# A graph network with experts: layer 0's experts from gathered lanes instead of all tokens, and smaller edits beside it

## The chip, the cores and the metric

One core of one Trainium2 chip runs the whole program. The time is device microseconds (us) of one execution; the median of five runs stands for a kernel. Engines are named as in the profile: PE (matrix), PEld (its weight loads), DVE (vector), ACT (scalar), POOL (GpSimd), SP (issues DMAs).

## The reference

N = 3125 nodes with 256 features, E = 50000 edges sorted by destination, all in f32. Four pairs of a graph layer and an expert layer, each added to x. What matters here is the first pair, the first graph half of the second, and the experts of layers 2 and 3:

```
x = x + gnn0(LN(x))      # sum over edges of (h @ W[relation])[src] * weight, by dst
x = x + ffn0(LN(x)):     # 8 experts, each token keeps its best 2
    logits = t @ router.T ; rw, re = top_k(softmax(logits), 2) ; rw = rw / rw.sum
    out = t + sum over the 2 chosen e of rw_e * (gelu(t @ w1[e] + b1[e]) @ w2[e] + b2[e])
x = x + gnn1(...):       # msg = embed[type][src] * (edge_feats @ W_dist) * cutoff ; summed by dst
x = x + ffn2(...)        # 16 experts of 256->512->256, best 2 of 16
x = x + ffn3(...)        # 8 experts of 256->512->256, best 2 of 8
```

## The kernel before

The program has stages. **Stage one** (`stage_one`, 98 to 1892 us of the profile) does layer 0 and the graph half of layer 1 together, one tile of 126 nodes after another, 25 tiles. Then a small stage for layer 1's feed-forward (to 2110 us), layer 2's attention over edges with its 16 experts and the table for layer 3 (to 3197 us), layer 3's maximum over edges (to 3845 us), and layer 3's 8 experts (to the end).

In stage one a tile has 21 windows, each the edges of six nodes. `window` (L874 on) does, for window k: two matmuls of the gathered rows by a weighted 0/1 matrix s (L881, tile `c`, 96 columns), copied out by ACT to `aT` (L885), a matmul of edge features (L888, tile `pw`), and DVE's product `mt = pw * g` (L891), which lets go of the gathered row buffer `g`, of which there are nine; POOL then gathers row k+9 (L136, through the helper `gather`). `build` makes the two matrices of 0/1 columns two windows ahead on DVE: `s0` (L866, 96 wide, times the edge's weight) and `s1` (L868, 32 or 128 wide, times the edge factor of layer 1). `add_up` multiplies each `mt` by its `s1` into one PSUM tile `agg` (L907), which ACT copies to `ag` (L913). After the 21 windows, eight calls of `weigh` multiply `aT` by the relation weights (L920).

The order of work is written out by hand: the stage runs under a manual schedule, so every engine executes in the order of the program text. After each window and each `weigh` call stands one **slot**, `between()`: there are 29 slots a tile. In each slot the `Flow`s of finished pairs of tiles advance by a planned number of steps, and so do a list of background steps (`background`: edge offsets, node ranks for the later layers), weight loads and the zeroing of DRAM tables. A `Flow` has three parts, paced by slots:

```
PARTS = ((route, 22, 25), (experts, 32, 56), (combine, 34, 52))     # part, steps, slots
```

`route` normalises the pair's 2 x 126 tokens, turns them (L950, L951), takes the router's logits (L993) and the best two (`top2_steps`), and adds the second bias (L1012, L1013). `experts` runs **all eight experts on all 252 tokens**: a hidden layer in two halves of two matmuls each (L1029, 252 columns), gelu on ACT (L1031), then for each of the two tiles two matmuls of 256 columns (L1038), and DVE's x = py * comb + x (L1040), where comb is zero for an expert that was not chosen. `combine` does layer 1's graph half and writes the two tables for later layers. After the last tile the remaining Flows run out, one step a slot (the **tail**). All parts take their PSUM from one tag `w` with two buffers (`bank`).

`background` finds each tile's edge range: `begin(t)` gathers rows (POOL), and two slots later `starts` counts on DVE (L584, L586) and multiplies on PE at once (L651). Later it ranks the nodes: per tile three matmuls (L1347 to L1349) and a 0/1 matrix from DVE (L1325), then L1377 with four DVE-built operands (L1373, L1375).

For layers 2 and 3 a planner (`Plan`) orders each engine's instructions from estimated costs. `Experts.loads` issues on SP, expert by expert, the tokens' rows (`ro_x`, L1988) and the two halves of the expert's weights (`ro_w`, L1994, two buffers each); the rows of a chunk of tiles can only be loaded when all of its tokens have been scattered to DRAM (`xg`). `ex2.rest` is a branch for tokens beyond an expert's places (L2072). `attend` reads gathered neighbour rows from nine `g_rows` buffers.

Of the kernel before, what the change touches and what calls it, by code (L numbers as in the profile page):

```python
# [19 lines left out]
P = 128  # L20
# [58 lines left out]

def places(n, chunk):  # L80

    return n * chunk[2] * chunk[3]
# [9 lines left out]
BG_EVERY = 3  # L92


@with_exitstack
def tile_gnn_ffn(ctx: ExitStack, tc: tile.TileContext, a: dict, out: bass.AP):
# [214 lines left out]
    ex = dram.tile([NX, 2 * D], F32, name="ex")  # L311
    tabr = dram.tile([NX, VW], F32, name="tabr")
# [334 lines left out]
    def starts(t, n, pf):  # L647

        for i in range(t, t + n):
            find.count(i)  # L650
        nc.tensor.matmul(pf[:R1, :n], sel[:GC, :], startF[:GC, t : t + n], start=True, stop=True)  # L651
        nc.vector.tensor_scalar(mixI[:R1, t : t + n], pf[:R1, :n], off[:R1], None, op0=OP.add)
# [12 lines left out]
    for i in range(5):  # L665
# [9 lines left out]
        if i == 0:  # L675
            starts(0, 2, ps("tp", [P, 2]))
            first_meta = meta_load(0, wb)
# [39 lines left out]
    def first_zeros():  # L717
        exv = ex.rearrange("(p r) d -> p (r d)", p=TN)
        for c in range(0, NT * 2 * D, ET):
            nc.sync.dma_start(exv[:, c : c + ET], zero[:TN])  # L720
            yield
        nc.sync.dma_start(tab2[NX:, :], zero[: NP - NX, :ZW])
# [65 lines left out]
    def stage_one(late, cp, eb):  # L788
# [67 lines left out]
        def build():  # L856
            k = nxt["s"]
            if k < len(wins):
# [3 lines left out]
                s0 = eb.tile([P, GW], F32, name="s0", bufs=4)  # L862
                a = quarter(j)
                a, m1 = (0, P) if a is None else (32 * a, 32)
                s1 = eb.tile([P, m1], F32, name=f"s1_{m1}", bufs=13 if m1 == 32 else 3)
                nc.vector.tensor_scalar(s0, iota_f[:, :GW], m[:, F_CODE, j : j + 1], m[:, F_NORM, j : j + 1],  # L866
                                        op0=OP.is_equal, op1=OP.mult)
                nc.vector.tensor_scalar(s1, iota_f[:, a : a + m1], m[:, F_DST, j : j + 1], m[:, F_CUT, j : j + 1],  # L868
                                        op0=OP.is_equal, op1=OP.mult)
                sums[k] = s0, s1  # L870
# [3 lines left out]
        def window(k):  # L874
# [5 lines left out]
            for h in range(2):  # L880
                nc.tensor.matmul(pc[:, h, o : o + GW], g[:, h * P : (h + 1) * P], sums[k][0], start=True, stop=True)  # L881
# [8 lines left out]
            mt = mults[t, j] = eb.tile([P, D], F32, name="mt", bufs=11), sums.pop(k)[1]  # L890
            nc.vector.tensor_tensor(mt[0], pw, rows.pop(k)[:, D:], op=OP.mult)  # L891
            fetch_rows()

        ag_of, mults = {}, {}

        def add_up(t, b):
# [4 lines left out]
            for js in together[b]:  # L901
                js = [j for j in js if (t, j) in mults]
                for j in js:
                    a = quarter(j)
                    mt, s1 = mults.pop((t, j))
                    o = agg if a is None else agg[32 * a : 32 * a + 32]
                    nc.tensor.matmul(o, s1, mt, start=not begun, stop=(j == 10), skip_group_check=True)  # L907
                begun = True
            if b == 2:
                q, i = t // 2, t % 2  # L910
                if i == 0:
                    ag_of[q] = eb.tile([P, 2, D], F32, name="ag", bufs=3)
                nc.scalar.copy(ag_of[q][:TN, i, :], agg[:TN])  # L913

        def weigh(t, i):
# [6 lines left out]
            if i == 7:  # L922
                x = x_of[t // 2][:TN, t % 2, :]
# [3 lines left out]
        x_of, e_of = {}, {}  # L927
# [4 lines left out]
        def load_x(q):  # L932
            n = size(q)
            x = x_of[q] = eb.tile([P, 2, D], F32, name="x", bufs=3)
            if n == 1:
                nc.gpsimd.memset(x[:, 0, :], 0.0)
                nc.sync.dma_start(x[:TV, 0, :], a["x"][2 * q * TN :, :])
            else:
                nc.sync.dma_start(x[:TN], a["x"][2 * q * TN : 2 * (q + 1) * TN, :].rearrange("(t p) d -> p t d", p=TN))

        def load_e(q, i):
            n = size(q)
            e = e_of[q, i] = eb.tile([P, 2, D], F32, name=f"e{i}", bufs=1)
            nc.sync.dma_start(e[:TN, :n], rows126(ex, 2 * q, n)[:, :, i * D : (i + 1) * D])
# [29 lines left out]

        def route(q):

            n = size(q)
            x = x_of[q][:TN, :n, :]
            nc.vector.tensor_add(x, x, e_of.pop((q, 0))[:TN, :n])
            yield  # L980
            xn = eb.tile([P, 2, D], F32, name="xn0", bufs=1)[:TN]
# [1531 lines left out]
```

## Time and profile before

| | us |
|---|---|
| median of 5 runs (4242.15 to 4262.89) | 4250.05 |
| the profiled execution | 4246.1 |
| its span, first to last instruction | 4244.4 |
| PE busy, share of span | 2721.8, 64% |
| DVE busy | 1959.1, 46% |
| POOL busy | 1729.9, 41% |
| ACT busy | 851.5, 20% |
| TensorE clock granted, mean | 0.775 |

Busy times are unions of an engine's instructions; matmuls overlap, so the distance from one matmul's start to the next says more than its duration. An f32 matmul shows as two records (832 records of L1029 are 416 matmuls). Granted clock 1.00 is full speed and 0.50 half. In a group's row, "busy, mean ns of one | idle before it, and what ended that".

### The profile page before, as it was taken

The numbers are of one execution on the slowest core, as the hardware profiler recorded it, in microseconds if no ns is written. First come the engines' busy times: TensorE is split into PE (matmuls) and PEld (weight loads), VectorE is DVE, ScalarE is ACT, GpSimd is POOL, SyncE is SP. The second block draws the span as 40 slices with busy tenths as digits, with TensorE's granted clock in tenths as the row PEclk, the third lists the DMA queues.
The fourth block names the chain that finished last, engine by engine and source line by source line (L and its number), as shares of the span: only waits on it lengthen the run. The fifth ranks groups of instructions, "written<-read, shape, count | busy, mean of one in ns | idle before, by whom it ended". The sixth has DMA issues, their size and how long they took to land. (4 is left out here: it accounts for less than half of the span.)

```text
span 4244.4 us, 46833 instructions
## 1 busy us (share of the span) xinstructions
PE 2721.8 (64%) x13015; PEld 2151.1 (51%) x13015; DVE 1959.1 (46%) x7555; ACT 851.5 (20%) x1821; POOL 1729.9 (41%) x1971
## 2 busy tenths in 40 slices
PE   3678999988989999957512365456561111137885
PEld 2556777777778787746401244244441111125653
DVE  4445666665664555453344433534662332345300
ACT  2111232221222322221100021112220000013321
POOL 1332333431443333101366554544436666643323
PEclk9668999988899999977755576678775555556987
DMA  5756544532334444212233354354533333323553
GB/s 187 216 171 198 156 138 134 153 89 75 102 100 121 136 117 122 74 47 77 70 99 83 104 183 143 110 172 146 173 123 98 87 92 94 89 61 124 156 159 103
DMA packets 274480, 518.32 MB, mean 122 GB/s; under 512 B 53068, under 2 KB 176106, under 8 KB 274194
## 3 DMA queue, kind: packets, MB, share of 16 engines
q0 software_dynamic: 103744, 303.34, 24.5%
q1 hardware_dynamic: 159598, 201.27, 15.6%
q10 hardware_dynamic: 10852, 10.45, 0.8%
q8 instruction: 113, 1.85, 0.2%
q14 instruction: 173, 1.42, 0.1%
HBM read 428.07 MB, written 86.78 MB: 121 GB/s over the span
## 5 line engine op out<-in xcount | busy, mean ns | idle before, releaser
L136 POOL DMA_INDIRECT g<-tab,m_si x521 | 497.2, 954 | 1020.8 <-DVE mt L891 527.1
L136 POOL DMA_INDIRECT g_rows<-tab,srcI x413 | 400.3, 969 | 292.0 <-DVE ACC L2248 135.9
L136 POOL DMA_INDIRECT g_row<-tab,srcI x413 | 399.9, 968 | 190.2 <-issue 102.0
L881 PEld LDWEIGHTS c<-s,g 128*128 128x128 f32 x2084 | 347.6, 218 | 143.7 <-issue 67.7
L881 PE MATMUL c<-s,g 128*128 128x96 f32 x2084 | 357.2, 300 | 77.8 <-issue 29.0
L888 PE MATMUL pw<-w_d,f 65*128 65x256 f32 x1042 | 377.6, 448 | 13.5 <-DVE mt L891 11.0
L920 PE MATMUL f<-w_rel,aT 128*126 128x256 f32 x1600 | 379.1, 387 | 0.0
L1973 PE MATMUL mm<-ro_xt,ro_w 128*128 128x192 f32 (+3 forms) x1152 | 289.3, 400 | 132.8 <-ACT ro_h L2038 58.8
L885 ACT COPY aT<-c 128x384 f32<-128x384 f32 (+1 forms) x323 | 236.7, 737 | 604.5 <-PE c L881 445.9
L920 PEld LDWEIGHTS f<-w_rel,aT 128*126 128x126 f32 x1600 | 304.1, 192 | 51.5 <-issue 5.7
L1643 PE MATMUL tp<-ident,ACC 128*128 128x128 f32 x50 | 16.3, 429 | 473.7 <-DVE ACC L2368 457.8
L1973 PEld LDWEIGHTS mm<-ro_xt,ro_w 128*128 128x128 f32 x1152 | 212.6, 217 | 192.8 <-issue 72.1
L1977 PE MATMUL y<-ro_w,ro_h 128*96 128x256 f32 (+2 forms) x1152 | 287.2, 404 | 16.5 <-issue 13.6
L891 DVE TENSOR_TENSOR mt<-pw,g 128x256 f32<-128x256 f32 x521 | 218.7, 420 | 164.4 <-PE pw L888 92.9
L1643 PEld LDWEIGHTS tp<-ident,ACC 128*128 128x128 f32 x50 | 7.2, 202 | 481.9 <-issue 400.4
L1977 PEld LDWEIGHTS y<-ro_w,ro_h 128*96 128x96 f32 (+2 forms) x1152 | 210.3, 188 | 69.4 <-issue 17.5
L1038 PE MATMUL w<-w,b_h 128*126 128x256 f32 x800 | 219.1, 399 | 11.3 <-ACT xt L951 3.9
L1029 PE MATMUL w<-xt,w 128*128 128x252 f32 (+1 forms) x832 | 219.5, 389 | 3.6 <-ACT b_h L1031 1.3
L2248 DVE SCALAR_TENSOR_TENSOR ACC<-g_rows,g_e,ACC 128x256 f32<-128x256 f32 x413 | 201.0, 487 | 42.7 <-DVE ACC L2248 20.2
L140 POOL DMA_INDIRECT xg<-XX,ro_pos x100 | 100.9, 1009 | 288.9 <-issue 173.6
L2368 DVE TENSOR_TENSOR ACC<-ACC,g_row 128x256 f32<-128x256 f32 x413 | 173.4, 424 | 82.9 <-DMA g_row<-tab,srcI 64.2
L2215 PE MATMUL pu<-w_s,a_xt 128*128 128x256 f32 x100 | 46.4, 613 | 237.1 <-DVE ACC L2243 93.4
(582 smaller groups left out, 4710.6 us busy)
## 6 DMA issues: line engine op xcount, KB each, us to landing
ro_w<-in_L_ffn_blocks SPq DMA_DIRECT2D x72, 514.0 KB
ro_w<-in_L_ffn_blocks SPq DMA_DIRECT2D x72, 512.0 KB
f<-in_attr_t SPq DMA_DIRECT2D x521, 32.5 KB
xg<-zero SPq DMA_DIRECT2D x78, 200.0 KB
b_at<-in_edge_attr SPq DMA_DIRECT2D x100, 125.0 KB
tabr<-v SPq DMA_DIRECT2D x12, 758.0 KB
g<-tab,m_si POOLq DMA_INDIRECT x521
g_rows<-tab,srcI POOLq DMA_INDIRECT x413
```

The lines of the kernel that those rows point to most:

```text
L136: return nc.gpsimd.indirect_dma_start(out=dst, out_offset=None, in_=table, in_offset=bass.IndirectOffsetOnAxis(ap=idx, axis=0))
L881: nc.tensor.matmul(pc[:, h, o : o + GW], g[:, h * P : (h + 1) * P], sums[k][0], start=True, stop=True)
L885: nc.scalar.copy(aT[:, :, :, b : b + n * GN].rearrange("p k r n -> p k n r"), pc[:, :, : n * GW].rearrange("p k (n r) -> p k n r", r=16))
L888: nc.tensor.matmul(pw, feats.pop(k), wd, start=True, stop=True)
L891: nc.vector.tensor_tensor(mt[0], pw, rows.pop(k)[:, D:], op=OP.mult)
L920: nc.tensor.matmul(cur["f"][:TN], aT[:, h, r, :], wrel[:, h, r, :], start=(r == 0 and h == 0), stop=(r == 15 and h == 1))
L1029: nc.tensor.matmul(ph, w["01"][:, e, k, i * P : (i + 1) * P], xt[:, k, : n * TN], start=(k == 0), stop=(k == 1))
L1038: nc.tensor.matmul(py, last[:, k, i * TN : (i + 1) * TN], w["02"][:, e - 1, k, :], start=(k == 0), stop=(k == 1))
L1973: nc.tensor.matmul(ph, w[:, o : o + P], xt[:, k, :], start=(k == 0), stop=(k == 1))
L1977: nc.tensor.matmul(py, h[:, i, s], w[:, i * D : (i + 1) * D], start=(i == 0), stop=(i == self.fc - 1))
L2248: stt(u, g[:, r, :D], e[:, r0 + r : r0 + r + 1], u, op0=OP.mult, op1=OP.add)
L2368: nc.vector.tensor_tensor(u, u, rows.pop(r), op=OP.max)
```

## The change

1. `experts` on all tokens is gone, except for the last tile (`dense`, one tile). Instead `route` also ranks the chosen tokens of each expert, over chunks of two or three tiles (`CH0`, nine chunks), into 128 places per expert (`P0`), stores x and the sums to DRAM (`xs`), and scatters each token's normalised row twice into DRAM (`xg0`, POOL, four scatters a pair). `chunk` then loads 128 rows an expert (SP), turns them, runs the hidden layer with 128 columns and the output with 256, and stores the result (`yg0`, SP). `combine` loads x back from `xs`, gathers two rows for each token (POOL, four gathers a pair), and adds them with their weights (four DVE instructions); its rest is now `layer1`.
2. `Flow` is replaced by four `Lane`s (combine; combine of the last tile; chunks; route), with their own steps and slots, and waits of 3 slots between a lane's end and the start of what depends on it. A branch `rest0` for tokens beyond 128 places an expert stands after the tail.
3. `build` makes only `s0`, three ahead; `whose` makes the `s1` columns three times a tile: one comparison for four groups (four of these a tile), and five single ones. The edge factor moves into DVE's product at L891, which becomes a scalar_tensor_tensor.
4. `agg` is added by DVE into the x tile's second half, which is loaded from `ex` together with x; `first_zeros` copies x into `ex` and zeroes `xg0` as well.
5. `background`: counting is a slot ahead of the matmul at L651; the rank loop builds its 0/1 matrix one tile ahead and drops one of three matmuls; L1377's operands are built one tile ahead.
6. `Experts.loads` is split in two chains of the planner, `tokens` and `weights`; layer 2's last chunk takes the weights of experts 2 to 15 into the `g_rows` buffers, once the last neighbour gather has been issued.

```
+CH0 = (0, 3, 6, 9, 12, 15, 18, 20, 22, 24)
+P0 = 128
+R_STEPS, X_STEPS, C_STEPS = (33, 33), (29, 42), (40, 46)
...
-                nc.vector.tensor_scalar(s1, iota_f[:, a : a + m1], m[:, F_DST, j : j + 1], m[:, F_CUT, j : j + 1],
-                                        op0=OP.is_equal, op1=OP.mult)
...
-            nc.vector.tensor_tensor(mt[0], pw, rows.pop(k)[:, D:], op=OP.mult)
+            stt(mt, pw, mts[t][:, F_CUT, j : j + 1], rows.pop(k)[:, D:], op0=OP.mult, op1=OP.mult)
...
+        def whose(t, b):
+            m = mts[t][:, F_DST]
+            n = GL if t == NT - 1 else GC
+            for js in together[b]:
+                js = [j for j in js if j < n]
+                if b < 2:
+                    s1 = eb.tile([P, 4, 32], F32, name="s1g", bufs=4)
+                    of = m[:, js[0] : js[-1] + 1 : 5].unsqueeze(2).to_broadcast([P, len(js), 32])
+                    nc.vector.tensor_tensor(s1[:, : len(js)], iota_f.rearrange("p (q n) -> p q n", n=32)[:, : len(js)],
+                                            of, op=OP.is_equal)
...
             if b == 2:
-                nc.scalar.copy(ag_of[q][:TN, i, :], agg[:TN])
+                g = xa_of[t // 2][:TN, t % 2, D:]
+                nc.vector.tensor_add(g, g, agg[:TN])
...
+            for i in range(2):
+                t = 2 * q + i
+                c = AT0[t]
+                for k in range(2):
+                    if k or i:
+                        nc.gpsimd.memset(gap, 0.0)
+                    scatter(xg0[c % 3], pos[:TN, k, t : t + 1], xn[:, i, :D], f"xg0_{c}")
+                    yield
+        def hidden0(e, xt, n, h):
+            for i in range(2):
+                ph = bank()[:, 0, :n]
+                for k in range(2):
+                    nc.tensor.matmul(ph, w["01"][:, e, k, i * P : (i + 1) * P], xt[:, k, :n], start=(k == 0), stop=(k == 1))
+                nc.scalar.activation(h[:, i, :n], ph, AF.Gelu, bias=w["b01"][:, 2 * e + i : 2 * e + i + 1])
+        def out0(py, e, h):
+            for k in range(2):
+                nc.tensor.matmul(py, h[:, k, :], w["02"][:, e, k, :], start=(k == 0), stop=(k == 1))
+        def chunk(c):
...
+            load(0)
+            load(1)
+            yield
+            yield
+            yield
+            for e in range(10):
+                if e < 8:
+                    pt, x = bank()[:, :, :P], xe.pop(e)
+                    for k in range(2):
+                        nc.tensor.transpose(pt[:, k, :], x[:, k * P : (k + 1) * P], ident)
+                    xt[e] = eb.tile([P, 2, P], F32, name="c_xt", bufs=1)
+                    nc.scalar.copy(xt[e], pt)
+                    load(e + 2)
+                    store(e - 2)
+                    yield
...
+                if 1 <= e < 9:
+                    py = bank()[:, 0, :]
+                    out0(py, e - 1, h.pop(e - 1))
+                    y[e - 1] = eb.tile([P, D], F32, name="c_y", bufs=2)
+                    nc.scalar.copy(y[e - 1], py)
+                    yield
...
+                if e < 8:
+                    h[e] = eb.tile([P, 2, P], F32, name="c_h", bufs=2)
+                    hidden0(e, xt.pop(e), P, h[e])
+                    yield
...
+        lanes = [
+            Lane([job("C", q, ("X", AT0[2 * q + 1]), 3, combine, C_STEPS) for q in range(last)]),
+            Lane([job("C", last, ("X", last), 0, combine, C_STEPS)]),
+            Lane([job("X", c, ("R", (CH0[c + 1] - 1) // 2), 3, chunk, X_STEPS) for c in range(len(CH0) - 1)]
+                 + [job("X", last, ("R", last), 0, dense, (16, 32))]),
+            Lane([job("R", q, ("F", q), 0, route, R_STEPS) for q in range(last + 1)]),
+        ]
...
             for i in range(t, t + n):
                 find.fetch(i)
             yield
+            yield
+            for i in range(t, t + n):
+                find.count(i)
             yield
             starts(t, n, tp(n))
...
-            sel = chosen(t)
+            sel, nxt = nxt, (chosen(t + 1) if t + 1 < NT else None)
             pk = tp(P)
-            nc.tensor.matmul(pk, ones[:1, :], base[:1, :], start=True, stop=False)
-            nc.tensor.matmul(pk, ones, prev, start=False, stop=False)
+            nc.tensor.matmul(pk, ones, prev, start=True, stop=False)
...
-            pl.add(0, ex2.loads())
+            pl.add(0, ex2.tokens())
+            pl.add(0, ex2.weights((blocks, lambda: gp.tile([P, GB, ZW], F32, name="g_rows", bufs=GR_BUFS)
+                                   .rearrange("p r d -> p (r d)"), here[order2[-1]])))
```

## The prediction

> **What bounds the kernel now.** I read the busy shares by stage first. The columns are the stretch, its length, busy time of PE, PEld, DVE, ACT, POOL (instructions), granted clock, DMA share, GB/s; the stretches are my cuts: stage one up to tile 3, tiles 4 to 16, tiles 17 to 24, the tail, then layer 2's last chunk of experts, then layer 3's experts.
>
> ```profile
> 97.60:427.70 330.10, 254.67 (x1067) 195.66 (x1067) 162.99 (x603) 51.05 (x77) 110.47 (x117) 0.74 0.64 196
> 427.70:1328.00 900.30, 830.15 (x4397) 679.26 (x4398) 560.20 (x2335) 222.18 (x411) 321.51 (x361) 0.92 0.42 118
> 1328.00:1784.70 456.70, 441.05 (x2545) 368.04 (x2543) 244.18 (x995) 133.56 (x250) 155.05 (x163) 1.00 0.42 118
> 1784.70:1892.50 107.80, 74.32 (x323) 54.93 (x324) 50.97 (x242) 29.42 (x75) 0.15 (x1) 0.85 0.15 49
> ...
> 3003.00:3197.00 194.00, 133.17 (x618) 101.52 (x618) 115.81 (x436) 57.26 (x160) 76.03 (x99) 0.79 0.50 161
> ...
> 3845.00:4244.40 399.40, 301.18 (x1249) 218.93 (x1249) 102.13 (x462) 120.89 (x242) 122.16 (x179) 0.84 0.46 141
> ```
>
> From 428 to 1785 us PE works 94% of the time (1271 of 1357 us), the next engine (DVE) 59%. PE bounds stage one, so PE time removed there is time won, unless the order makes PE wait. Single tiles say how sharply (a late tile; two in which nodes are ranked):
>
> ```profile
> 1444.40:1500.50 56.10, 55.09 (x324) 47.26 (x323) 28.36 (x111) 16.41 (x29) 21.01 (x22) 1.00 0.42 118
> 927.20:1035.80 108.60, 97.23 (x500) 76.39 (x499) 66.36 (x305) 18.35 (x35) 21.02 (x22) 0.91 0.26 73
> 1035.80:1119.90 84.10, 76.18 (x354) 61.43 (x353) 47.37 (x204) 16.37 (x29) 27.48 (x29) 0.82 0.30 80
> ```
>
> A late tile has PE idle for 1.0 of 56.1 us; POOL has 35 us of room in it, DVE 28. For prices I take distances between starts in PE's timeline (start, length, instruction):
>
> ```profile
> 1500.33 0.62 PE L888 MATMUL pw<-w_d,f 65*128 65x256 f32 x2
> 1500.79 1.01 PE L1029 MATMUL w<-xt,w 128*128 128x252 f32 x4
> 1501.64 0.58 PE L881 MATMUL c<-s,g 128*128 128x96 f32 x4
> ...
> 1503.70 1.03 PE L1038 MATMUL w<-w,b_h 128*126 128x256 f32 x4
> 1504.57 0.58 PE L881 MATMUL c<-s,g 128*128 128x96 f32 x4
> 1504.98 0.62 PE L888 MATMUL pw<-w_d,f 65*128 65x256 f32 x2
> ```
>
> Half a hidden layer of 252 columns costs 0.85 us (1500.79 to 1501.64), one tile's output 0.87 (1503.70 to 1504.57), the four records of 96 columns 0.42: cost goes with columns, so 128 columns cost 0.43. Two transposes (L950, 1514.68 to 1514.90) cost 0.22.
>
> **1. Layer 0's experts on PE.** Before: an expert and pair costs 2 x 0.85 + 2 x 0.87 = 3.44. Pair 11's route fills the last 25 slots, so pairs 0 to 10 have their experts inside the tile loop: 11 x 8 x 3.44 = 303 us. After: an expert and chunk costs 2 x 0.43 + 0.87 + 0.22 = 1.95. Chunk 7 ends 33 + 3 + 42 = 78 slots after tile 21, 83 being left, so chunks 0 to 7 are in the loop: 8 x 8 x 1.95 = 125. That is **-178** at full clock. Of it, tiles 4 to 16 have 13 tiles of 13.8 less four chunks of 15.6, 117, at clock 0.92: **-10** more. Ranking adds two small matmuls a pair, 4 records of 0.1 as in L993 (8 records of 8 columns from 1523.97 to 1524.77), 12 pairs: **+5**.
>
> **2. Other engines under that cover.** DVE: the 0/1 columns were 521 x 0.31 (L868, 308 ns) and become 225 of 0.30 (a 128x128 comparison; row L1331, 295 ns): -95. The product becomes a scalar_tensor_tensor; nearest row L1040, from PSUM, 0.483 against 0.420: +33. Those of the experts go from 200 to 56: -70. Some 22 small route operations a pair at 0.17 (rows of 126x16, 153 to 181 ns): +45. The `agg` addition +11, two wide additions -16. Sum -92. ACT: gelu and `ag` -105, 160 gelu of 0.36 and 144 copies of 0.37 +111: +6. POOL: 96 scatters and gathers, 0.97 each with 0.3 between (row L140): +122 over the stage, in its idle time. Each is nothing on the path while PE is the longest; without that cover POOL's cost is 122.
>
> **3. Waits that go.** PE waits for the range counts at L651:
>
> ```profile
> PE w L651 <- DVE startF L586: 28.4, 7, 5.7
> ...
> PE w L651 <- DVE q_rows L584: 4.2, 2, 2.6
> PE w L651 <- issue: 3.6, 1, 3.6
> ```
>
> (us in total, times, longest.) Together 36.2 us in the first 430, and the clock there is 0.74. A slot's delay takes PE out of this wait; DVE still stands up to 2.3 us for the gathered rows (204.26), which PE meets later at `s0` or `pw`. I take **-28**; ends 0 and -50 (with the clock). The rank loop loses L1347, 13.0 us busy (50 records), and L1377's operands come one tile earlier, of whose waits (20.0) a third goes, since four comparisons of 0.29 a tile still pace it: **-20**; ends -5 and -35.
>
> **4. Waits that come.** The lanes put more and shorter work into the same two PSUM buffers: a chunk's step has two hidden halves of 0.43 each ahead of gelu's 0.36, where it was one of 0.85 ahead of 0.47. Behind a waiting PE instruction stand the windows of the next tile, and DVE and POOL wait for those. SP now waits for scatters before the chunk's loads, for PE before each next one, and for ACT before each store; behind it stand the `f` loads, six windows (some 10 us) ahead. POOL waits for route's positions and for SP's stores; behind it stand gathers nine windows ahead (15 us). Four scatters in four slots need 4 x 2.5 us of POOL against 4 x 1.8, so it falls 3 us behind, inside that cover and roughly inside the 3 slots' wait. No row shows the new order. From below: DVE is lighter, idle time falls by 1 us a tile, -20. From above: tiles 13 to 16 show 5 to 8 us idle where late ones show 1 to 3, so 5 us on 22 tiles, +110. I take 2 us a tile, nearer the late tiles, since most of stage one has no more DVE or POOL work than they can hide: **+45**.
>
> The clock goes with this. Columns as above, 3.4 us each side of a wait of 1.64 us at L881:
>
> ```profile
> 669.20:672.60 3.40, 1.76 (x10) 1.50 (x10) 3.23 (x15) 0.87 (x1) 1.47 (x2) 1.00 0.48 139
> 672.60:679.40 6.80, 6.80 (x24) 5.92 (x23) 5.39 (x27) 2.80 (x6) 4.87 (x6) 0.50 0.78 207
> ```
>
> PE idle for 1.64 of 3.4 us was followed by 6.8 us at half clock; shorter waits in the late tiles were not. The Trainium skill ("TensorE: Matmul & The Clock Gate", section "HAM oscillation — how this bites in real kernels") states as the rule that gaps must not pass some 3.4 us; this row is stricter, and by the page's rule new waits of 1 us would cost only themselves, about +22 in place of +45. The same page, section "A second HAM failure mode: psum-queue depth-cycling", speaks against this change: PE that idles briefly between groups of matmuls while it cycles through PSUM buffers can swing between half and full clock; by it the sum would come near the slower rival below.
>
> **5. Tail and branch.** By my count of the lanes the tail has 97 single steps where it had 102 (route, chunk, combine in line); its 108 us go down by 6 for that and for less PE work, but four DMA trips (scatter, load, store, gather) come into its chain. The branch is priced by L2072: 4.5 us at 2996, 12.9 at 3998. I take -6 and +6, **0**; ends -25 and +35.
>
> **6. Layers 2 and 3.** The last chunk of layer 2 runs 16 experts from 3003 to the last store at 3136, 8.3 us each, while its PE work is 3.7 (2 x 8 records of 0.108, 8 of 0.217, transposes 0.22) and its weights 1.05 MB come at 161 GB/s, 6.5 us. In the new order 13 halves of weights stand before the branch, so the chunk can go some 45 us faster. The table's work on DVE (116 us busy of 194) then is late next: **-20**; ends +5 and -45. In layer 3 the first weights no longer wait for tokens, but the experts there are PE work of 11 us: **-5**; ends +10 and -15.
>
> **The sum.** -178 - 10 + 5 - 28 - 20 + 45 + 0 - 20 - 5 = -211. Against the profiled execution, 4246 - 211 = 4035; that one lies 4 under the median of five (4250.05), so 4039, rounded to **4040**.
>
> **Rivals.** (a) The lanes wait: point 4 at its upper end and layer 2 bound by DVE, +65 + 20 + 20 for the tail: about 4145 (4100 to 4230). For it speak the tiles with idle 5 to 8 us when chains through DVE grow; against it the late tiles. (b) The starved stretches recover: point 4 at -20, layer 2 at -45: 3950 to 3990; for it speaks clock 0.74 to 0.92 before 1328. (c) **Slower**: the clock. In tiles 4 to 24, PE with a tenth less work idles 1.6 us in a 3.4 us stretch in nearly every slot group and stays at half clock. Tiles 4 to 16 lose 0.08 x 900 = 72 us to it now; to eat 211 us, 422 us more must run at half clock, a mean clock near 0.8 over the stage, where the late tiles have 1.00. From there it is 4263 and more. (d) The places overflow and the branch runs 24 tiles with all experts, at least 24 x 13.8 = 330 us more than 4040; the reference's inputs put at most 111 tokens of a chunk on one expert, 128 fit: 1 in 100.
>
> **Chances.** Forecast (3990 to 4100) 0.55, (a) 0.22, (b) 0.12, slower by (c) or (d) 0.08, no change 0.03. Faster 0.89, same 0.03, slower 0.08; 0.3% (13 us) is about what a measurement of this kernel tells from no change. The range leaves out the outer parts of (a) and (b) and all that is slower: 3965 to 4160.
>
> **What would show it.** Late tiles near 50 us with PE idle under 4; no PE wait at L651's line; the two rank tiles shorter by some 20; the last layer-2 chunk under 100 us. Wrong if late tiles stay at 55 or more, or the stage's clock falls under 0.9 after tile 4.

## The result and the profile after

The change made no difference on the chip of the forecast: 4259.53 us against 4252.35 for the kernel before, ratio 1.0009, 95% interval 0.9998 to 1.0020. The forecast of 4040 (3965 to 4160) was wrong. The profiled execution takes 4249.0 us, its span is 4247.3 (before 4246.1 and 4244.4), and the mean granted clock falls from 0.775 to 0.739.

One thing must be known before the experiments are read. Their runs fell on chips of two kinds. Beside `a_pw3`, `e_pw3`, `a_fill` and `a_pre` the kernel before takes 4249.8 us, as in the runs that the forecast and the result rest on; beside all others it takes 3788.2 to 3791.6. I call them **a 4250 chip** and **a 3790 chip**. Ratios are always against the kernel before on the same chip. On a 3790 chip the change is worth 1.3% (0.9868), still not the forecast 5%.

The busy shares by stage, of the kernel after, with the columns of the forecast's first view. The rows are stage one to tile 3, tiles 4 to 16, tiles 17 to 24, the tail (to the first matmul of the next stage, which was 1892.5 before), layer 2's last chunk alone (the forecast's row holds the table for layer 3 too), layer 3's experts:

```profile
97.60:416.60 319.00, 245.98 (x995) 191.47 (x995) 147.18 (x551) 42.28 (x60) 119.36 (x128) 0.68 0.69 211
416.60:1300.60 884.00, 774.44 (x3980) 626.25 (x3981) 511.22 (x2192) 210.94 (x415) 373.18 (x403) 0.82 0.51 147
1300.60:1778.10 477.50, 430.21 (x2508) 354.23 (x2506) 230.35 (x998) 146.41 (x310) 189.39 (x230) 0.92 0.51 147
1778.10:1900.80 122.70, 74.93 (x320) 54.76 (x320) 51.54 (x262) 37.19 (x99) 13.09 (x16) 0.76 0.28 87
...
3023.50:3136.00 112.50, 96.08 (x517) 79.35 (x517) 77.55 (x286) 46.69 (x133) 49.43 (x61) 0.92 0.54 177
3850.00:4247.30 397.30, 296.99 (x1245) 217.00 (x1245) 100.83 (x452) 119.29 (x239) 122.26 (x179) 0.85 0.42 135
```

PE has fewer instructions in tiles 4 to 16 (3980 for 4397), and yet those tiles take 884.0 us for 900.3, because the clock is 0.82 for 0.92; tiles 17 to 24 are even longer than before (477.5 for 456.7), at 0.92 for 1.00.

To split such a row I count idle time as length less PE busy, lost time as half of the time in which PE was busy at granted clock 0.50 (132, 335, 67 and 273 us by the traces), and the rest as work at full clock. Tiles 4 to 24:

| | length | work at full clock | lost to the clock | idle |
|---|---|---|---|---|
| 4250 chip, before | 1357.0 | 1205 | 66 | 86 |
| 4250 chip, after | 1361.5 | 1037 | 168 | 157 |
| 3790 chip, before | 1284.0 | 1199 | 33 | 52 |
| 3790 chip, after | 1254.1 | 1030 | 137 | 87 |

The work went nearly as forecast, by 168 us on both chips. On the 4250 chip the clock took back 102 of it and idle time 71; on the 3790 chip 103 and 35. Outside these tiles, on the 4250 chip: first tiles -11, tail +15, layer 1's rest +3, layer 2 -7, layer 3 -1, which with +4.5 makes the 2.9 us by which the span grew.

Single tiles of the kernel after, same columns: a late tile in which a chunk runs for most of its length, one in which it runs for less, and two in which nodes are ranked:

```profile
1484.70:1539.90 55.20, 52.86 (x326) 43.79 (x326) 29.18 (x133) 18.22 (x40) 26.98 (x29) 0.97 0.65 195
1539.90:1600.50 60.60, 53.91 (x315) 44.55 (x314) 27.16 (x113) 18.57 (x39) 23.48 (x26) 0.92 0.46 130
985.10:1068.70 83.60, 71.05 (x395) 58.19 (x394) 49.54 (x220) 19.44 (x39) 23.57 (x27) 0.86 0.35 96
1068.70:1162.00 93.30, 81.59 (x392) 65.76 (x391) 57.05 (x273) 18.74 (x40) 31.01 (x33) 0.78 0.39 115
```

With 2 to 7 us idle these late tiles have lost the full clock. Where PE waits, by its waits in tiles 4 to 16 of the kernel after (us in total, times, longest):

```profile
PE pw L908 <- DVE mt L912: 45.1, 28, 5.5
PE pw L908 <- issue: 8.9, 5, 4.3
PE w L1659 <- DVE k_ohh L1649: 7.1, 14, 1.6
```

Line 908 is the matmul into `pw`, line 912 DVE's product that reads it: `pw` has two buffers, so window k waits for the product of window k-2. This wait was 3.3 us before. The pages' groups tell the same of the whole span (busy, mean ns of one, idle before it), first before, then after:

```profile
L888 PE MATMUL pw<-w_d,f 65*128 65x256 f32 x1042 | 377.6, 448 | 13.5 <-DVE mt L891 11.0
```

```profile
L908 PE MATMUL pw<-w_d,f 65*128 65x256 f32 x1042 | 427.7, 500 | 137.5 <-DVE mt L912 89.6
```

The same 1042 records wait ten times as long and each takes 500 ns for 448: the two losses in one row.

### The profile page after: what moved, and what is told of

Read it like the earlier page. It is cut to its first block, busy times and chain, and to the rows that moved or that the text cites. A ratio compares the mean times of both kernels' runs of the same rounds, so it can differ in the third digit from the quotient of the medians.

```text
span 4247.3 us, 46383 instructions
## 1 busy us (share of the span) xinstructions
PE 2652.1 (62%) x12486; PEld 2083.9 (49%) x12486; DVE 1883.1 (44%) x7430; ACT 854.0 (20%) x1893; POOL 1838.5 (43%) x2103
## 5 line engine op out<-in xcount | busy, mean ns | idle before, releaser
L908 PE MATMUL pw<-w_d,f 65*128 65x256 f32 x1042 | 427.7, 500 | 137.5 <-DVE mt L912 89.6
L901 PEld LDWEIGHTS c<-s,g 128*128 128x128 f32 x2084 | 381.3, 240 | 76.0 <-issue 37.7
L901 PE MATMUL c<-s,g 128*128 128x96 f32 x2084 | 388.5, 320 | 28.2 <-DMA w_b<-in_L_ffn_b 23.5
L912 DVE SCALAR_TENSOR_TENSOR mt<-pw,m_mt,g 128x256 f32<-128x256 f32 x521 | 250.0, 480 | 306.7 <-PE pw L908 140.4
L2255 PE MATMUL mm<-ro_xt,ro_w 128*128 128x192 f32 (+3 forms) x928 | 251.9, 423 | 149.0 <-ACT ro_h L2336 98.7
L2255 PEld LDWEIGHTS mm<-ro_xt,ro_w 128*128 128x128 f32 x928 | 181.6, 218 | 203.0 <-ACT ro_h L2336 104.5
L908 PEld LDWEIGHTS pw<-w_d,f 65*128 65x128 f32 x1042 | 201.2, 240 | 156.2 <-DVE mt L912 99.9
L2259 PE MATMUL y<-ro_w,ro_h 128*96 128x256 f32 (+2 forms) x1040 | 260.6, 406 | 17.3 <-issue 10.6
L2259 PEld LDWEIGHTS y<-ro_w,ro_h 128*96 128x96 f32 (+2 forms) x1040 | 189.5, 188 | 68.5 <-issue 15.3
L888 DVE TENSOR_SCALAR s<-iota_f,m_mt 128x96 f32<-128x96 f32 x521 | 175.6, 338 | 0.0
```

The source lines that it names most:

```text
L908: nc.tensor.matmul(pw, feats.pop(k), wd, start=True, stop=True)
L912: stt(mt, pw, mts[t][:, F_CUT, j : j + 1], rows.pop(k)[:, D:], op0=OP.mult, op1=OP.mult)
L2255: nc.tensor.matmul(ph, w[:, o : o + P], xt[:, k, :], start=(k == 0), stop=(k == 1))
L2259: nc.tensor.matmul(py, h[:, i, s], w[:, i * D : (i + 1) * D], start=(i == 0), stop=(i == self.fc - 1))
```

## The experiments

**Theories.** The main one: PE's work was the bound only while other work kept it busy. Taken away, it leaves PE idle for a microsecond here and there; the granted clock then falls, and the slower clock takes the gain. Rivals: the lanes' DMAs on POOL cost what they save; the lanes run unevenly, so some tiles have too little work and others too much; the two `pw` buffers alone make the wait; or the 0/1 columns, the background and the loads give the loss back.

**1. The two kernels again, and the change in parts.** `before_again` and `after_again` are the two kernels on a 3790 chip. `e_ones` is the kernel before with part 3 of the change alone, `e_bg` with part 5 alone, `e_all3` with parts 3, 5 and the loads of part 6: all that doesn't concern the lanes. `a_lanes` is the opposite, the kernel after with these edits undone; parts 1, 2 and 4 remain.

> The kernel before, unchanged, for its profile: the last four kernels ran on a chip on which it takes 3788 us and not 4252. If it lands on such a chip again: tiles 17 to 24 at 56 and 60 us as in the first profile (PE-bound there), tiles 4 to 16 some 30 to 50 us shorter, layer 2's attention near 640 us where it was 893, and no product on VectorE that starts over 1 us after its matmul's recorded end while VectorE waits for it (37 of 118 waiting products did in the first profile).

> The changed kernel, unchanged. If what ate its gain are PE's results that reach VectorE and ScalarE late (57 of 169 waiting products in its first profile), then on a chip without these the gain is there: 150 us less than before or more. If the lanes' own order eats it (the scatters and gathers cost 54 us by the last call, the uneven chunk work some more), the gain stays small on both chips: 0 to 40 us less than before here, 0 to 15 more than before on a chip like the first.

> The kernel before with one edit alone: one comparison makes four groups' 0/1 columns, and the edge factor moves into VectorE's product. By my terms it is hidden (62 us of VectorE time off an engine that is not the bound): 0, at most 15 less. If VectorE's stretches of work in front of the product are what PE waits for, 20 to 35 less.

> The kernel before with the background edits alone (range counts a slot ahead, ranks and the two-column loop a tile ahead, one matmul less): by my terms 28 + 20 = 48 less. The rival: the wait moves from the counts to the product in the first tiles, and only the ranking gains: 10 to 25 less.

> The kernel before with the edits that do not concern the lanes: grouped 0/1 columns with the edge factor in the product, the background edits (counts a slot ahead, ranks and the two-column loop a tile ahead, one matmul less), and layer 2's and 3's loads in two generators. By my terms 28 + 20 + 20 + 5 = 73 us less, about 4180. The rival, read from the stages of the changed kernel (first tiles 11 us earlier, layers 2 and 3 some 8 us shorter), gives 4230 to 4240.

> The other edits without the sparse experts, unchanged from the first call (0.988 of before there). Where before takes 3788: the same, 0.986 to 0.990. Where it takes 4250: if the edits are worth as much there, 4200 and the sparse experts cost 50 to 60 us on that chip.

> The sparse experts alone: the changed kernel with the old 0/1 columns and product, the old background, and the old loads of layers 2 and 3. By my terms 1, 4 and 5 it would be 138 us faster than before; by what has been measured since (all other edits together give what the whole change gives) the sparse experts are worth nothing: within 10 us of before on a chip with before near 3788, 10 to 40 us slower than before where it takes 4250.

`before_again` is one execution of 3782.6 us, some 8 under the median of the kernel before; its tiles 4 to 16 are 62 us shorter than on the 4250 chip.

| run, 3790 chips | us | ratio to before [95%] |
|---|---|---|
| after_again | 3742.7 | 0.9868 [0.9832, 0.9904] |
| e_ones | 3775.3 | 0.9960 [0.9940, 0.9980] |
| e_bg | 3762.9 | 0.9920 [0.9899, 0.9942] |
| e_all3 | 3741.2 | 0.9879 [0.9851, 0.9906] |
| e_all3_again | 3747.9 | 0.9880 [0.9863, 0.9896] |
| a_lanes | 3796.5 | 1.0012 [0.9999, 1.0025] |

The lanes alone, which carry 178 of the 211 us forecast, are worth nothing; the small edits make the whole 1.2%. `e_ones` and `e_bg` multiply to 0.988, which leaves part 6 little, though layer 2 takes 823 us in `e_all3` for 845 in `before_again`; the intervals are too wide to settle that. So no side edit gave a gain back: that rival falls. Tiles 4 to 16 and 17 to 24 of `before_again`:

```profile
418.00:1256.50 838.50, 794.47 (x4416) 659.02 (x4415) 558.32 (x2340) 223.81 (x413) 322.98 (x362) 0.96 0.43 127
1256.50:1702.00 445.50, 437.44 (x2538) 366.49 (x2537) 246.88 (x996) 133.77 (x251) 154.65 (x163) 1.00 0.41 122
```

and of `after_again`:

```profile
411.40:1235.10 823.70, 749.85 (x3981) 613.01 (x3982) 511.14 (x2192) 217.72 (x415) 375.29 (x403) 0.84 0.53 157
1235.10:1665.50 430.40, 417.10 (x2508) 348.16 (x2506) 231.32 (x998) 151.61 (x310) 190.38 (x230) 0.95 0.53 163
```

Here idle time explains little (PE is busy 91% and 97% of these rows); the clock, 0.84 for 0.96, explains most. (This profiled execution is the slowest of its four, 3755.1 us for a median of 3742.7.) In `after_again` the late tiles that carry a chunk reach the forecast (48.3, 49.8, 52.4, 49.8 and 51.0 us, idle at most 0.4 and in the last 2.3); those between two chunks do not (65.0 us at clock 0.82, 65.4 at 0.87). The same three stretches of `a_lanes`, to tile 3, tiles 4 to 16 and 17 to 24:

```profile
97.60:436.50 338.90, 248.18 (x991) 186.65 (x991) 163.95 (x625) 42.75 (x60) 118.65 (x128) 0.65 0.66 203
436.50:1275.00 838.50, 772.04 (x4035) 620.82 (x4036) 529.53 (x2359) 217.16 (x415) 374.75 (x430) 0.84 0.52 153
1275.00:1693.40 418.40, 410.09 (x2508) 340.21 (x2506) 236.26 (x1055) 152.44 (x310) 187.76 (x203) 0.98 0.56 168
```

So "worth nothing" is a sum: against `before_again` the lanes gain 27 us in tiles 17 to 24, nothing in tiles 4 to 16, and lose some 20 in the first tiles, where the forecast had no cost for them, and 14 in the tail.

`after_again` also answers a rival of the 4250 chip: had results that reach DVE late (part 5 below) eaten the gain, 150 us or more should have come back on a chip without them. It was 48, near the 0 to 40 of the other forecast.

**2. How much is PE work worth?** Three kernels leave work out. `b_half` is the kernel before with layer 0's experts on the first tile of each pair only; `b_noexp` leaves all of its expert matmuls, gelu and sums out; `a_nochunk` is the kernel after whose chunk loads and stores its rows but turns and multiplies nothing.

```
b_half
-    nc.tensor.matmul(ph, w["01"][:, e, k, i * P : (i + 1) * P], xt[:, k, : n * TN],
+    nc.tensor.matmul(ph, w["01"][:, e, k, i * P : (i + 1) * P], xt[:, k, :TN],
...
     for i in range(n):
+        if i:
+            yield
+            continue
b_noexp
-    nc.tensor.matmul(ph, w["01"][:, e, k, i * P : (i + 1) * P], xt[:, k, : n * TN],
...
-    nc.tensor.matmul(py, last[:, k, i * TN : (i + 1) * TN], w["02"][:, e - 1, k, :],
...
-    stt(x[:TN, i, :], py, comb_of[q][:TN, i, e - 1 : e], x[:TN, i, :], op0=OP.mult, op1=OP.add)
a_nochunk
-    xe[e] = eb.tile([P, D], F32, name="c_x", bufs=2)
+    xe[e] = eb.tile([P, D], F32, name="c_x", bufs=6)
...
-    for k in range(2):
-        nc.tensor.transpose(pt[:, k, :], x[:, k * P : (k + 1) * P], ident)
...
+    xt[e] = xe.pop(e)
...
-    out0(py, e - 1, h.pop(e - 1))
...
+    y[e - 1] = h.pop(e - 1)
...
-    hidden0(e, xt.pop(e), P, h[e])
+    h[e] = xt.pop(e)
```

> The kernel before, in which layer 0's experts run only on the first of each pair's two node tiles (the second tile's expert sums are left out), in the same order and the same number of steps; nothing is added. That takes 8 x 1.72 us of PE work from each of 11 pairs, 151 us, a little less than the 178 of the forecast, and no new transfer or wait comes in. Three theories. Traffic: what ate the gain is the transfers that the lanes add (scatters, gathers, stores, loads); then this kernel gains nearly all of it, about 4110 (4090 to 4140). Unevenness: what ate it is that PE has chunk work in 42 of 87 slots and only short windows in the others, where PE waits and its clock halves; here the work stays evenly spread, so 4110 to 4160. Next bound: the windows' chain through DVE, ACT and the row gathers could not go faster than some 55 us a tile in any case; then this kernel stays at 4220 or more.

> The kernel before without layer 0's experts in the tile loop and in the tail (their matmuls, gelu and sums are left out for all pairs): 303 us of PE work less in the loop and some 28 in the tail, nothing added. With half of it gone the stage up to tile 24 was 67 us shorter for 151 us of work. PE bound: 303 to 330 us faster than before. Clock and chain: PE's slots get shorter than VectorE's and the results' way, PE idles and its clock halves; the second half of the work brings less than the first, so 100 to 160 us faster in the stage and 28 in the tail, 130 to 190 in all.

> The changed kernel without the chunks' PE and ACT work (transposes, hidden layers, outputs and their copies are left out, loads and stores stay): 125 us of PE work less in the loop, 16 in the tail. PE bound: 125 to 140 us faster than the changed kernel. Clock and chain: 20 to 70 us faster, the mean clock of tiles 4 to 24 at or under 0.86.

| run, 3790 chips | us | ratio [95%] | PE work left out | gain |
|---|---|---|---|---|
| b_half | 3704.2 | 0.9785 [0.9751, 0.9819] | 151 (of before) | 84 |
| b_noexp | 3647.6 | 0.9622 [0.9606, 0.9638] | 331 (of before) | 144 |
| a_nochunk | 3736.0 | 0.9843 [0.9826, 0.9861] | 141 (of after) | 9 against 0.9868 |

The first 151 us pay 84, the next 180 pay 60, and the last 141 of the kernel after pay 9 with intervals that overlap; both theories had asked for more of it (20 to 70, or 125 to 140). Work taken from PE there no longer shortens the stage. Tiles 4 to 16 and 17 to 24 of `a_nochunk`:

```profile
416.00:1237.60 821.60, 742.55 (x3532) 592.82 (x3533) 511.49 (x2192) 170.38 (x286) 373.96 (x403) 0.76 0.54 158
1237.60:1664.20 426.60, 397.20 (x2061) 318.13 (x2060) 230.42 (x999) 105.87 (x182) 190.02 (x230) 0.85 0.56 165
```

It has 900 instructions fewer than `after_again` in these rows, the same length within 6 us, and a clock of 0.76 and 0.85. Time at half clock between 410 and 1690 us: 78 us in `before_again`, 319 in `after_again`, 549 in `a_nochunk`. How a stretch of it begins and ends, in `a_nochunk`:

```profile
1400.60:1404.00 3.40, 0.36 (x2) 0.36 (x3) 1.88 (x9) 0.00 (x0) 1.26 (x2) 1.00 0.96 305
1404.00:1427.90 23.90, 23.70 (x86) 17.71 (x85) 10.38 (x44) 4.87 (x9) 11.93 (x13) 0.50 0.74 227
1427.90:1434.70 6.80, 6.80 (x35) 5.36 (x34) 3.35 (x17) 0.00 (x0) 0.59 (x1) 1.00 0.32 102
```

PE idles for 3.0 of 3.4 us; then it is busy for 23.70 of 23.90 us and still stays at half clock; the full clock is back some ten records after the dense 128x256 matmuls of the relation weights have begun. What fills the stretch are mostly the windows' matmuls of 96 columns, and of 65 rows by 256. The Trainium skill ("TensorE: Matmul & The Clock Gate", section "Part 1: The HAM clock gate (the "warmup" mystery)") gives about 3.4 us of sustained activity as what restores the full clock; this row has seven times that and does not restore it, so the measurement decides: busy in the trace is not enough.

**3. Does work added to PE bring the clock back?** If so, PE's idle time and thin matmuls are the cause, and filler should cost less than its own time. Both kernels are the kernel after with filler in the 265 slots that have no chunk step. `a_fill` does the 96-column products twice (+0.42 us each, 111 us at full clock), on the 4250 chip, and `a_fill_again` on a 3790 chip; `a_dense` adds one 128x256 product into `pw`, which the window's own matmul then overwrites (+0.46 each, 122 us).

```
a_fill, a_fill_again
-    for h in range(2):
+    for h in range(2) if cur.get("chunk") else (0, 1, 0, 1):
...
+    cur["chunk"] = lanes[2].gen is not None
a_dense
+    if not cur.get("chunk"):
+        nc.tensor.matmul(pw, ident, wrel[:, 0, 0, :], start=True, stop=True)
...
+    cur["chunk"] = lanes[2].gen is not None
```

> The changed kernel in which, in each slot without chunk work, PE does the first product of the window (the four records of 96 columns, 0.42 us) twice, with the same result. That is about 250 windows x 0.42 = 105 us of added PE work and no other change. Theory 'clock': PE is not the bound in these slots, its waits and its halved clock are; the filler takes the place of waiting and keeps the clock up, so the time stays within 20 us of the changed kernel or falls below it, and the mean clock of tiles 4 to 24 rises from 0.88 to 0.93 or more. Rival 'PE bound': 80 to 105 us slower.

> The short filler once more, beside the dense one: the window's four records of 96 columns twice in the same 265 slots, 111 us more PE work. On the slower of the two chips it cost 64 of them and half clock stayed at 355 us. Theory 'dense columns': 50 to 90 us slower than the changed kernel (0.987 of before on the faster chip, 1.001 on the slower), at least 40 slower than the dense filler. Rival 'busy share': within 20 us of the dense filler.

> The changed kernel with a filler in the 265 slots without chunk work: one matmul more of 128 rows by 256 columns into the pw buffer, which the window's own product then overwrites. PE gets 265 x 0.46 = 122 us more to do. Theory 'dense columns': half clock, once begun, lasts until long dense matmuls run (in the kernel without chunk work 20 to 24 us of windows with PE busy 0.98 to 0.99 stayed at half clock and it ended some 8 records into the node terms); then this filler ends it sooner, half-clock time in tiles 4 to 24 falls from 280 us to under 150, and the time stays within 30 us of the changed kernel, far under what the filler costs. Rival 'busy share': only idle time counts, so the dense filler does what the short one (a_fill_again) does, and both are equally slow.

`a_fill`: 4313.7, 1.0159 [1.0108, 1.0210], 54 us more than the kernel after took in the result (64 by the ratios): neither forecast held (at most 20 more by the one, 80 to 105 by the other). `a_fill_again`: 3773.3, 0.9946 [0.9924, 0.9968], 30 more than `after_again` (forecast 50 to 90). `a_dense`: 3732.9, 0.9849 [0.9828, 0.9869], 7 to 10 less than `after_again`, within the intervals. So 122 us of dense matmuls cost nothing, while 111 us of thin ones cost 30; both figures are of a 3790 chip, and the dense filler was not run on the 4250 chip. `a_dense`, tiles 4 to 16 and 17 to 24:

```profile
419.50:1221.70 802.20, 744.35 (x4266) 621.41 (x4267) 512.05 (x2193) 217.75 (x415) 373.53 (x403) 0.93 0.55 161
1221.70:1652.50 430.80, 419.21 (x2580) 354.17 (x2578) 232.53 (x998) 151.06 (x310) 190.26 (x230) 0.98 0.55 163
```

Its clock is back at 0.93 and 0.98 (`a_fill_again`: 0.89 and 0.98), its time at half clock at 147 us (198, from 319), and tiles 4 to 16 take 802.2 us for 823.7 although PE does more. Some 180 of the 265 fillers, 82 us, stand in these two rows, and still they are 21 us shorter than in `after_again`. That the clock takes what the lanes save is thus shown, on a 3790 chip, by adding work. That the columns of a matmul count beside its time is the simplest reading of 147 against 198; PE's idle time differs little between the two (57.8 + 11.6 and 53.3 + 11.8).

**4. Where PE's idle time comes from.** `a_nodma` is the kernel after without the lanes' scatters and gathers on POOL (experts then read stale rows, `combine` adds rows of the x tile). `a_even` spreads each chunk over more slots. `a_pw3` and `e_pw3` give `pw` a third buffer on the kernel after and on `e_all3`, by letting `agg` and the relation sums share one PSUM bank, and with that the results change. `a_pre` loads the edge attributes of layer 2 one block earlier, with three buffers for two.

```
a_nodma
-    scatter(xg0[c % 3], pos[:TN, k, t : t + 1], xn[:, i, :D], f"xg0_{c}")
...
-    g = to[:TN, k, :D]
+    g = xa[:TN, i, D:]
...
-    gather(g, yg0[AT0[t] % 3], back[:TN, k, t : t + 1])
a_even
+X_SPAN = (84, 84, 84, 84, 74, 46, 54, 42, 42)
...
-    Lane([job("X", c, ("R", (CH0[c + 1] - 1) // 2), 3, chunk, X_STEPS) for c in range(len(CH0) - 1)]
+    Lane([job("X", c, ("R", (CH0[c + 1] - 1) // 2), 3, chunk, (29, X_SPAN[c])) for c in range(len(CH0) - 1)]
a_pw3, e_pw3
-    psums(c0=2, pw=2, agg=1, f0=1, w=2):
+    psums(c0=2, pw=3, agg=1, w=2):
...
-    cur["agg"] = ps("agg", [P, D])
+    cur["af"] = ps("agg", [P, 2, D])
+    cur["agg"] = cur["af"][:, 0, :]
...
-    cur["f"] = ps("f0", [P, D])
+    cur["f"] = cur["af"][:, 1, :]
a_pre
-    at = eb.tile([EP, AB, 64], F32, name="b_at", bufs=2)
+    at = eb.tile([EP, AB, 64], F32, name="b_at", bufs=3)
...
-    if b:
-        old, b0 = prev
+    due.append((at, b))
+    if len(due) == 3 or b is None:
+        old, b0 = due.pop(0)
```

> The changed kernel without the scatters of tokens and without the gathers of expert outputs on POOL's queue (the chunks compute on zero rows, and the weighted sums read a tile that is there already); loads, stores, PE, ACT and DVE work are the same. Traffic theory: PE idle in tiles 4 to 24 falls from 157 us to about 90 and the half clock with it, time 4190 or less. Unevenness and next bound: 4240 to 4260, since the chunk work stands where it stood.

> The changed kernel with each chunk's steps spread over nearly all slots up to the next chunk (84, 84, 84, 84, 74, 46, 54, 42, 42 slots in place of 42 each); nothing else is changed. Unevenness theory: no stretches without chunk work are left, so PE idles less, the mean clock over tiles 4 to 24 goes from 0.86 to 0.93 or more, time 4200 or less. Traffic and next bound: the same transfers and the same chain, 4245 to 4265.

> The changed kernel with three PSUM buffers for the edge weights (pw) in place of two; the bank comes from the sums (agg) and the node terms (f), which now share one. PE may run three windows ahead of VectorE's product in place of two. Theory 'stretches': with less PE work in a slot, VectorE's stretches of small work ahead of a product (up to 7 us) last longer than two windows, PE waits at pw (53 us of waits, none of 0.5 us or more in the kernel before) and its clock halves (about 320 us at half clock in tiles 4 to 24, against 70); then the third buffer takes away a good part of the waits, and the time falls 25 to 80 us below the changed kernel. Rival 'PE bound': waits at pw are a result, not a cause; within 10 us of the changed kernel, or slower by the waits of the shared bank (up to 0.6 us a tile, 15 us).

> The same third pw buffer in the kernel that has the old dense experts and the other edits. There PE never waits at pw for 0.5 us or more, so both theories expect no gain: within 10 us of that kernel (0.988 of before on the chip where before takes 3788), at most 15 slower by the shared bank.

> The changed kernel in which the background's edge attributes (b_at) are loaded two blocks ahead in place of one (three buffers for two). VectorE waits 48 us for them in tiles 4 to 24 where the kernel before waits 18, and the longest of PE's waits at pw (7.2, 4.4 us) stand behind such a load. Theory 'stretches': 10 to 30 us faster than the changed kernel. Rival: no change, within 6 us.

| run | chip | us | ratio [95%] |
|---|---|---|---|
| a_nodma | 3790 | 3724.2 | 0.9831 [0.9809, 0.9854] |
| a_even | 3790 | 3778.8 | 0.9982 [0.9958, 1.0006] |
| a_pw3 | 4250 | 4241.0 | 0.9969 [0.9946, 0.9992] |
| e_pw3 | 4250 | 4218.9 | 0.9934 [0.9908, 0.9960] |
| a_pre | 4250 | 4235.4 | 0.9958 [0.9933, 0.9984] |

Unevenness falls as a cause: with `a_even` stage one's tiles end at 1666.7 us as in `after_again` (1665.5), with 324 us at half clock (319), and the tail is 32 us longer. The lanes' DMAs may be a part of it: without them the kernel is 14 us faster by the ratios (18 by the medians), with intervals that overlap; the forecast had them at nothing. In the profiles those tiles end 40 us earlier (1625.2), but there the fastest of `a_nodma`'s executions stands against the slowest of `after_again`'s. `e_pw3`, which has no lanes, stands at 0.9934 where `a_pw3`, which has them, stands at 0.9969: on the 4250 chip too the lanes gain nothing.

The wait for the product, in `after_again` where it sums to 53.3 us in 38 waits (in `before_again` PE's idle time at this matmul is 0.0), goes back to DVE: DVE's own waits in tiles 4 to 24 have

```profile
DVE b_at L1551 <- DMA b_at<-in_edge_attr: 48.4, 25, 7.2
DVE q_rows L598 <- DMA q_rows<-dsr,k_rowi: 23.8, 16, 3.8
```

for, in `before_again`,

```profile
DVE b_at L1276 <- DMA b_at<-in_edge_attr: 18.1, 13, 3.6
DVE q_rows L584 <- DMA q_rows<-dsr,k_rowi: 12.9, 11, 3.7
```

DVE executes in the order of the program text, so a product behind such a wait is late, and PE two windows later. But neither cure moved tiles 4 to 24 on the 4250 chip, though both kernels are faster than the kernel after, clear of the intervals (0.9969 and 0.9958 for 1.0009, some 17 and 21 us). `a_pw3` cut PE's idle time at `pw` from 94.0 to 16.0 us, and PE then waited elsewhere (18.1 us for `aT`, 10.6 at the `agg` bank); tiles 4 to 16 took 883.6 us (884.0) at clock 0.83 (0.82). So on this chip the two `pw` buffers alone don't make the loss. Where its 17 us lie the profiles don't tell. `a_pre` gained in the first tiles (they end at 401.2 us for 416.6); its tiles 4 to 16 take 884.7 us, and 17 to 24 487.0 for 477.5. Nor could it show more there: on the 4250 chip DVE's wait for `b_at` in tiles 4 to 24 is 11.0 us after and 9.8 before, so what grew on the 3790 chip did not grow on this one. Neither was tried on a 3790 chip, so which of DVE's chains starts the idle time there was argued from the waits, not shown.

**5. What sets the two kinds of chips apart.** On the 4250 chip, DVE and ACT sometimes get PE's results late. From the kernel after (start, length, instruction, idle before it and releaser):

```profile
1429.85 0.62 PE L908 MATMUL pw<-w_d,f 65*128 65x256 f32 x2
...
1434.62 0.87 ACT L905 COPY aT<-c 128x384 f32<-128x384 f32 x1 [2.48 <-remote]
1435.18 0.95 POOL L145 DMA_INDIRECT g<-tab,m_si  x1 [0.30 <-issue]
1436.07 0.48 DVE L912 SCALAR_TENSOR_TENSOR mt<-pw,m_mt,g 128x256 f32<-128x256 f32 x1 [4.60 <-remote]
...
1436.61 1.22 PE L908 MATMUL pw<-w_d,f 65*128 65x256 f32 x2 [4.39 <-issue]
```

The matmul ends at 1430.47 by the record; its product, matched by order among 521 of each, starts at 1436.07, after 4.60 us of waiting, and PE, whose matmul after next needs the same buffer, idles for 4.39. Of the products of tiles 4 to 24 for which DVE waited over 0.1 us, 37 of 118 start over 1 us late in this way before, 57 of 169 after, by up to 11.6 us; on a 3790 chip none of 90 before and of 152 after. Of the late ones, 19 of 37 and 27 of 57 come free within 0.12 us of a recorded landing (of any piece) of a DMA that POOL issued; of the others only 12 of 81 and 20 of 112 do. These traces hold a third of the landing records of a 3790 chip's (1185 for 3521 on one semaphore of the kernel before), so the count is rough. More gathers and more waits for the product give more such delays, and that fits the larger idle loss here (71 us for 35). No run takes the delay itself away, so why it happens, and whether it makes the 460 us between the chips, stays open.

## Why the prediction was wrong, by its own steps

1. **Experts -178, ranking matmuls +5: nearly right.** Work at full clock fell by 168 us in tiles 4 to 24, where these terms and the removed rank matmul (13.0) make 186.
2. **The clock, -10: this is the step that failed.** The forecast took the lost time as a share of PE's work that would shrink with it. It grew by 102 us on the 4250 chip and by 103 on a 3790 chip. Rival (c) had the mechanism, with a chance of 0.08; its "mean clock near 0.8" was 0.85 over tiles 4 to 24, since it gave the whole 211 us to the clock and idle time took 71 of what was lost. What the forecast had against it, late tiles at clock 1.00, was made by the very expert work that the change removes: `a_nochunk` (0.76) and `a_dense` (0.93) show the clock follow the amount and the shape of the work left. The Trainium skill ("TensorE: Matmul & The Clock Gate", section "A second HAM failure mode: psum-queue depth-cycling"), weighed in the forecast as speaking against the change, points the same way: time at half clock went from 78 to 319 us on a 3790 chip. That the two PSUM buffers are the reason is not shown: a third one left the clock of tiles 4 to 16 at 0.83 (`a_pw3`).
3. **Other engines at 0.** Over stage one DVE went down by 79 us (forecast 92), ACT stayed (forecast +6), POOL went up by 108 (forecast 122). The amounts were nearly right. The price of nothing for POOL is in doubt: without the lanes' POOL work the kernel is 14 to 18 us faster, with intervals that overlap (`a_nodma`).
4. **Waits that go, -28 and -20.** The first 430 us of the kernel after show the wait moved on to the product, as this step itself considered:

```profile
PE pw L908 <- DVE mt L912: 34.9, 14, 9.7
...
PE w L663 <- DVE startF L600: 10.7, 6, 3.0
...
PE w L663 <- DVE q_rows L598: 1.8, 1, 1.8
PE w L663 <- PEq L764: 0.8, 1, 0.8
```

   Line 663 was L651; its wait fell from 36.2 to 13.3, not to none, and the wait at `pw` for DVE rose from 3.7 to 34.9: those tiles gained 11. The rank edits gave nothing in tiles 12 to 14 (`e_bg`: 254.1 us for 250.7).
5. **Waits that come, +45.** Idle time rose by 71 us, inside the bounds of -20 to +110; by 35 on a 3790 chip. The late tiles that this value was nearest to are the ones that keep PE busy: between chunks nothing does.
6. **Tail 0, layer 2 -20, layer 3 -5.** The tail measured +15, inside its end of +35. The chunk of layer 2 went from 125.4 to 110.7 us instead of under 100, and half of that was given back in the layer (-7); layer 3 gave -1. On a 3790 chip layer 2 was nearer to the -20: 11 us shorter in `after_again`, 22 in `e_all3`.

The prediction gave as its signs of being wrong "if late tiles stay at 55 or more, or the stage's clock falls under 0.9 after tile 4". Both came true.

## What to carry to other kernels

PE time removed is won only while PE stays busy without it: before pricing a removal at full clock, ask which work keeps the clock up and what stands in its place in each stretch. A cheap probe is to leave the work out altogether (here 141 us for 9) and to add dense matmuls in the gaps (122 us for nothing); if both do nothing to the time, PE's work is not what sets it. The same program on another chip can differ by more than the change, so ratios are taken on one chip.

## What was not expected of the hardware

Half clock lasted through 23.70 of 23.90 us of busy PE on thin matmuls. The same program took 3790 us on some chips and 4250 on another; layer 2's attention takes 893 us on the 4250 chip and 648 on a 3790 one with the same POOL work (471.7 and 474.3 us busy). When two running sums share one PSUM bank the results change (`a_pw3`); how stays open. Of all runs that leave nothing out, `a_dense`, with 122 us of useless matmuls, has the lowest ratio (0.9849 [0.9828, 0.9869]), though its interval overlaps those of the kernel after and of `e_all3`.
